# RWKV block with a split-precision feed-forward: the first tile's receptance input mixed ahead of its matmuls, tables loaded early, steps reordered

## The chip, the cores and the metric

The kernel runs on one core of a Trainium2 chip. The metric is device time in microseconds (us), the median of several runs. Beside the timed runs there is one profiled execution; all views of engines, waits and chains come from it.

## The reference, cut to what matters

`x` is 2 sequences of 4096 tokens with 256 features. A layernorm (without gain or bias) feeds a token-mixing attention, its result is added to `x`, a second layernorm feeds a feed-forward network, and that is added too.

```python
x_prev = jnp.pad(x[:, :-1, :], ((0, 0), (1, 0), (0, 0)))      # the token before
xk = x * time_mix_k + x_prev * (1.0 - time_mix_k)             # xv, xr alike
k = xk @ W_k.T; v = xv @ W_v.T; r = sigmoid(xr @ W_r.T)
# per token, with log-max state p and numerator q:
new_p = maximum(p, u + k_t)
scale_old = exp(maximum(p - new_p, -30)); scale_cur = exp(maximum(u + k_t - new_p, -30))
wkv_t = (scale_old * q + scale_cur * v_t) / (scale_old + scale_cur + 1e-9)
new_p2 = maximum(p + w, k_t)
q = exp(maximum(p + w - new_p2, -30)) * q + exp(maximum(k_t - new_p2, -30)) * v_t
y = r * wkv;  x = x + y @ W_o.T
# feed-forward of the second layernorm, width 1024, ternary weights with a scale per row:
h = silu(x2 @ w1.T * s1) * (x2 @ w2.T * s2)
h = gelu(h @ h1.T * sh1); h = gelu(h @ h2.T * sh2)
x = x + h @ w3.T * s3
```

## The kernel before, in words

Features lie on the 128 partitions (two blocks of 128, `ND = 2`), tokens on the free axis, in 16 tiles of 512 tokens. `split_block` does the work; `general_block` runs only if some feed-forward weight is not exact in the reduced format, which is tested on the way (`compare`) and isn't so here.

The feed-forward (`ffn`, lines 553 to 599) takes each input as the sum of a high and a low part (`hi`, `lo`), so that every product is two matmuls (lines 172 and 173). For tile i its steps are interleaved with the attention of tile i + 1 and the first layernorm of tile i + 2, generators that the loop at lines 608 to 624 advances step by step. A scheduler puts the emitted instructions into one queue per engine; every engine runs its queue in order. `tc.issue_after` ties an instruction behind another one.

The first tile has nothing to run beside, and so `first_tile` (lines 399 to 545) is written for latency, with the order on TensorE, VectorE and ScalarE fixed by hand: `on(engine, ...)` (line 340) puts every operation behind the one before on the same engine. Nearly all its operations therefore carry line 342. Its stages are:

- the first layernorm by halves of 256 tokens (`first_layernorm`, line 364), with dummy matmuls (`keep_warm`, line 356, output `unread`) in between;
- the token mix. It isn't applied to the tokens but to the weights: `scale` (line 431) makes, for k, v and r, copies `ws` of the 256x256 matrix whose rows are multiplied by the mix (`vec`) and by one minus the mix (`unmix`), four activations of 128x256 for each of the three. `project` (line 447) then needs four fp32 matmuls for each block: two with the tokens (`now`) and two with the tokens shifted by one (`then`);
- `differences` (line 464): a scan for the log-max (`state<-vec,state,ps_k`), and the exponents' arguments, clamped at line 472; `scales` (475): exp, relu, exp; two sigmoids for the shares `so`; a sigmoid of r; `state` (480): the numerator's scan and the two shares of the result;
- `y`, the output projection `ps_o`, the residual sum in `x_sb`, the second layernorm, and the split of `x2` into `x_hi` and `x_lo`, with which the feed-forward of tile 0 can start (its first matmul is `pa` at line 172).

Into this the steps of the second tile's first layernorm (`second = normalise(1)`) are placed by hand, one `next(second)` each: step 1 adds the halves and folds (`both` at line 187, a shift `folded` on ScalarE at 189), step 2 is the fold on VectorE (192) and `parts` on ScalarE (194), step 3 `parts` on VectorE (197), step 4 the averaging matmul (201), step 5 the subtraction (212), step 6 the variance, and so on. Step 1 also issues tile 2's load on GpSimd's queue. Steps 1 to 4 lie in `first_tile` (lines 491, 495, 508, 530), steps 5 and 6 in the feed-forward loop at steps 1 and 7, the rest at step 8 (lines 612 to 617).

GpSimd's queue issues the weight loads. After those of `w1`, `w2` and `h1` come eight copies of `h2` from HBM to HBM (line 123, 512 KB each), and the load of `w3` (124); behind these are the small copies `prev`, `log_max` and `numer` of the state that tile 1 needs (lines 445, 473, 484).

Of the kernel before, what the change touches and what calls it, by code (L numbers as in the profile page):

```python
# [13 lines left out]
P = 128  # L14
# [51 lines left out]
def split_block(ctx, tc, flags, x, vecs, w_attn, w1, w2, h1, h2, w3, out):  # L66
# [52 lines left out]
    h2_hbm = dram.tile([NH, P, NH, P], F32R, name="h2_hbm")  # L119
    for sb, src in ((w1_sb, w1), (w2_sb, w2), (h1_sb, h1)):  # L120
        nc.gpsimd.dma_start(out=sb, in_=src)
    for f in range(NH):
        nc.gpsimd.dma_start(out=h2_hbm[f], in_=h2[:, :, f * P : (f + 1) * P])
    nc.gpsimd.dma_start(out=w3_sb, in_=w3)

    mean_w = const.tile([P, P], F32, name="mean_w")
    vector.memset(mean_w, 1.0 / D)
# [209 lines left out]
    def behind(engine):  # L337
        return tc.issue_after(last[engine].ins) if engine in last else nullcontext()

    def on(engine, operation, *args, **kwargs):  # L340
        with behind(engine):
            last[engine] = getattr(getattr(nc, engine), operation)(*args, **kwargs)  # L342

    def matmul(*args, **kwargs):
        on("tensor", "matmul", *args, **kwargs)

    def activation(*args, **kwargs):
        on("scalar", "activation", *args, **kwargs)

    def add(out, a, b, op=ALU.add):  # L350
        on("vector", "tensor_tensor", out, a, b, op)

    def load_sqrt_table():
        activation(root, eps, AF.Sqrt)

    def keep_warm(unread, n, size=TS):

# [6 lines left out]
    def first_layernorm(src, xc, means):  # L364

        sq = wide.tile([P, ND, TS], F32, tag="wide", name="sq")
        for mean, p in zip(means, halves):
            for h in range(ND):  # L370
                add(xc[:, h, p], src[:, h, p], mean, ALU.subtract)
            activation(sq[:, :, p], xc[:, :, p], AF.Square)
        varis = []
        for p in halves:
            add(sq[:, 0, p], sq[:, 0, p], sq[:, 1, p])
            var = ps_ffn.tile([P, TS // 2 // P], F32, tag="pf", name="var")
            for b in range(TS // 2 // P):
                t = slice(p.start + b * P, p.start + (b + 1) * P)
                matmul(var[:, b : b + 1], sq[:, 0, t], mean_w[:, 0:1], start=True, stop=True)
            varis.append(var)  # L380
        yield
        spread = []
        for var in varis:
            each = tmp.tile([P, TS // 2 // P], F32, tag="each", name="each")
            activation(each, var, AF.Sqrt, bias=eps)
            on("vector", "reciprocal", each, each)
            rstd = ps_ffn.tile([P, TS // 2], F32, tag="pf", name="rstd")
            for b in range(TS // 2 // P):
                matmul(
                    rstd[:, b * P : (b + 1) * P], each[:, b : b + 1].to_broadcast([P, P]), ident, start=True, stop=True  # L390
                )
            spread.append(rstd)
            yield
        for rstd, p in zip(spread, halves):
            for h in range(ND):
                add(xc[:, h, p], xc[:, h, p], rstd, ALU.mult)
            yield

    def first_tile(second):
# [13 lines left out]
                    both = one.tile([P, 2, TS], F32, tag=tag, name="scale")  # L413
                    scales.append([both[:, k, :] for k in range(2)])

        load_sqrt_table()
        unread = ps_sum.tile([P, TS], F32, tag="ps", name="unread")
        keep_warm(unread, 8)
        means = []
# [6 lines left out]
        norm = first_layernorm(x_sb, xn, means)  # L426


        scaled = [[hid.tile([P, ND, D], F32, tag=tag, name="ws") for tag in ("hi", "lo")] for m in range(3)]

        def scale(m, *which):
            for k, c in which:
                j = m * ND + c
                activation(scaled[m][k][:, c, :], wa_sb[:, m, c, :], AF.Copy, scale=(vec, unmix)[k][:, j : j + 1])

        next(norm)
        scale(0, (0, 0))
        next(norm)
        scale(0, (1, 0))
        next(norm)  # L440
        scale(0, (1, 1), (0, 1))
        for m in range(1, 3):
            scale(m, (0, 0), (1, 0), (1, 1), (0, 1))
        run(norm)
        nc.gpsimd.tensor_copy(prev, xn[:, :, TS - 1 :])

        def project(m, h, kind, p=whole):
            pool, tag = kind
            ps = pool.tile([P, p.stop - p.start], F32, tag=tag, name="ps_" + "kvr"[m])
            now, then = (ws[:, :, h * P : (h + 1) * P] for ws in scaled[m])  # L450
            skip = 1 if p.start == 0 else 0
            shifted = slice(p.start + skip - 1, p.stop - 1)
            matmul(ps, now[:, 0, :], xn[:, 0, p], start=True, stop=False)
            for c in range(ND):
                matmul(ps[:, skip:], then[:, c, :], xn[:, c, shifted], start=False, stop=False)
            matmul(ps, now[:, 1, :], xn[:, 1, p], start=False, stop=True)
            return ps
# [6 lines left out]
        def differences(h):  # L464
            w, u = col(DECAY, h), col(FIRST, h)
            for k, p in keys[h]:
                t, after = lm[h][:, p], lm[h][:, p.start + 1 : p.stop + 1]
                on("vector", "tensor_tensor_scan", after, w.to_broadcast([P, p.stop - p.start]), k,
                   lm[h][:, p.start : p.start + 1], ALU.add, ALU.max)
                on("vector", "scalar_tensor_tensor", sc[h][1][:, p], t, w, k, ALU.add, ALU.subtract)  # L470
                on("vector", "scalar_tensor_tensor", so[h][1][:, p], k, u, t, ALU.add, ALU.subtract)
            on("vector", "tensor_scalar", sc[h][0], sc[h][1], NEG_CLAMP, 0.0, ALU.max, ALU.min)
            nc.gpsimd.tensor_copy(log_max[:, h : h + 1], lm[h][:, TS:])

        def scales(h):
            activation(sc[h][0], sc[h][0], AF.Exp)
            activation(sc[h][1], sc[h][1], AF.Relu)
            activation(sc[h][1], sc[h][1], AF.Exp, scale=-1.0)

        def state(h):  # L480

            on("vector", "scalar_tensor_tensor", sc[h][1], sc[h][1], MIN_SCALE, v[h], ALU.max, ALU.mult)
            on("vector", "tensor_tensor_scan", num[h][:, 1:], sc[h][0], sc[h][1], num[h][:, 0:1], ALU.mult, ALU.add)
            nc.gpsimd.tensor_copy(numer[:, h : h + 1], num[h][:, TS:])
            for share, of in zip(so[h], (num[h][:, 0:TS], v[h])):
                on("vector", "scalar_tensor_tensor", share, share, MIN_SHARE, of, ALU.max, ALU.mult)
            add(so[h][0], so[h][0], so[h][1])

        differences(0)
        with behind("vector"), behind("scalar"):  # L490
            next(second)
        last["vector"], last["scalar"] = marks["both"], marks["shift"]
        scales(0)
        with behind("vector"), behind("scalar"):
            next(second)
        last["vector"], last["scalar"] = marks["fold"], marks["hi"]
        differences(1)
        scales(1)
        for h in range(ND):
            activation(so[h][0], so[h][1], AF.Sigmoid, scale=-1.0)  # L500
            activation(so[h][1], so[h][1], AF.Sigmoid)
        for h in range(ND):
            activation(r[h], r[h], AF.Sigmoid)
            state(h)
        load_sqrt_table()

        with behind("vector"):
            next(second)
        last["vector"] = marks["split"]
        y = wide.tile([P, ND, TS], F32, tag="wide", name="y")  # L510
        add(y[:, 0, :], so[0][0], r[0], ALU.mult)
        for p in halves:
            add(y[:, 1, p], so[1][0][:, p], r[1][:, p], ALU.mult)
        banks = [
            [pool.tile([P, TS // 2], F32, tag=tag, name="ps_o") for pool, tag in kinds]
            for kinds in ((attn, attn), (attn, ffn))
# [6 lines left out]
        for ps_of, p in zip(banks, halves):  # L523
# [2 lines left out]
                add(x_sb[:, h, p], x_sb[:, h, p], ps_of[h])  # L526
                matmul(mean, mean_w, x_sb[:, h, p], start=h == 0, stop=h == ND - 1)
            means.append(mean)
        with behind("tensor"):
            next(second)  # L530
        last["tensor"] = marks["average"]
        unread = ps_attn.tile([P, TS], F32, tag="pa", name="unread")
        keep_warm(unread, 4)
        x2 = wide.tile([P, ND, TS], F32, tag="wide", name="x2")
        x2_hi = one.tile([P, ND, TS], F32R, tag="x2_hi", name="x2_hi")
        x2_lo = one.tile([P, ND, TS], F32R, tag="x2_lo", name="x2_lo")
        norm = first_layernorm(x_sb, x2, means)
        for _ in range(3):
            next(norm)
        keep_warm(unread, 6)  # L540
        run(norm)
# [63 lines left out]
    normal, got = {}, {}  # L605
    second = normalise(1)
    first_tile(second)
    for i in range(len(tiles)):
        ahead = attention(i + 1) if i + 1 < len(tiles) else iter(())
        further = normalise(i + 2) if i + 2 < len(tiles) else iter(())  # L610
        for step, _ in enumerate(ffn(i, *got.pop(i))):
            if i == 0:
                if step in (1, NH - 1):
                    with tc.issue_after(marks["rounded"].ins), tc.issue_after(marks["rest"].ins):
                        next(second)
                elif step == NH:
                    run(second)

            for _ in range(0 if step < NH else 4 if step == NH + (i == 0) else 1):
                next(ahead, None)  # L620
            if step > 2 * NH - 6 and step % 2 == 0:
                next(further, None)
        run(ahead)
        run(further)
# [287 lines left out]
```

## Time and profile before

| what | us |
|---|---|
| median of the timed runs (3) | 1572.11 |
| lowest and highest | 1571.52 and 1572.32 |
| the profiled execution, its own time | 1574.68 |
| its span | 1572.9 |
| PE busy | 1559.1 (99%) |
| DVE, ACT, POOL busy | 1102.0, 1034.4, 62.0 |
| first feed-forward matmul of tile 0 starts at | 45.14 |

PE is TensorE's matmuls, PEld its weight loads, DVE VectorE, ACT ScalarE, POOL GpSimd, SP SyncE. A line of the timeline gives start, duration, engine, source line, operation, output and inputs with their shapes, and in brackets the idle time before it and what ended it. A line of the chain gives start, duration, engine, output name and source line; it is followed back from the last instruction, so it shows who held up whom. The span starts at 0; a few us of the execution's own time lie outside it (1574.68 less 1572.9 is 1.8).

### The profile page before, as it was taken

What the parts mean: (1) busy time and instruction counts of PE and PEld (TensorE: products, weight loads), DVE (VectorE), ACT (ScalarE), POOL (GpSimd) and SP (SyncE); (2) the same over time, 40 slices, a digit from 0 to 9 for tenths busy, and PEclk for the clock granted to TensorE, in tenths of its full rate; (3) what the DMA queues carried; (4) which work ended last, traced back from release to release, by engine and by line L of the source; (5) the groups of instructions that cost most, each with busy time, mean ns of one, the idle gap of its engine ahead of it and who ended that gap; (6) DMA issues with size and microseconds to landing.
All of it is one profiled execution on the core that took longest, in us unless ns stands there. A gap on an engine that the chain in (4) does not pass through costs nothing.

```text
span 1572.9 us, 16652 instructions
## 1 busy us (share of the span) xinstructions
PE 1559.1 (99%) x6319; PEld 1185.9 (75%) x6319; DVE 1102.0 (70%) x1763; ACT 1034.4 (66%) x1394; POOL 62.0 (4%) x99
## 2 busy tenths in 40 slices
PE   9999999999999999999999999999999999999997
PEld 5768777777777778777787777877777787777886
DVE  6788686776768767786786867767687676865521
ACT  5676767667577585776767666675776857756542
POOL 3000000000000000000000000000000000000000
PEclk9999999999999999999999999999999999999999
DMA  9102031220402204021130311203112030211202
GB/s 360 42 32 103 14 121 34 73 88 9 130 30 75 79 20 134 14 90 65 34 121 14 107 48 47 94 14 108 41 64 78 21 108 27 80 48 34 94 14 69
DMA packets 36598, 109.16 MB, mean 69 GB/s; under 512 B 3680, under 2 KB 12384, under 8 KB 36000
## 3 DMA queue, kind: packets, MB, share of 16 engines
q1 hardware_dynamic: 19136, 67.93, 13.0%
q0 software_dynamic: 16960, 39.59, 8.1%
q8 instruction: 51, 0.84, 0.2%
q10 hardware_dynamic: 416, 0.52, 0.1%
q14 instruction: 35, 0.29, 0.1%
HBM read 99.64 MB, written 12.58 MB: 71 GB/s over the span
## 4 chain that ended last, share of the span: by engine, by line
PE 80%; issue 15%; DVE 2%; ACT 1%; DMA 1%; POOL 0%; POOLq 0%; DVEq 0%
PE ph L172 24%; PE ph L173 24%; PE pb L172 3%; PE pa L172 3%; PE pb L173 3%; PE pa L173 3%; PE po L173 3%; PE po L172 3%; PE ps_k L165 3%; PE ps_r L165 3%; PE ps_v L165 3%; PE ps_o L165 3%; PE mean L201 1%; DVE scale L342 0%; PE var L201 0%
## 5 line engine op out<-in xcount | busy, mean ns | idle before, releaser
L172 PE MATMUL ph<-hi,h_sb 128*128 128x512 f32 x2048 | 813.8, 397 | 0.0
L173 PE MATMUL ph<-lo,h_sb 128*128 128x512 f32 x2048 | 801.4, 391 | 0.0
L172 PEld LDWEIGHTS ph<-hi,h_sb 128*128 128x128 f32 x2048 | 384.9, 188 | 92.7 <-issue 11.7
L173 PEld LDWEIGHTS ph<-lo,h_sb 128*128 128x128 f32 x2048 | 385.0, 188 | 88.6 <-issue 8.4
L583 DVE TENSOR_TENSOR lo<-full,hi 128x512 fp32r<-128x512 f32 x256 | 175.4, 686 | 174.7 <-ACT full L582 173.6
L580 ACT ACTIVATE hi<-ph,vec 128x512 fp32r<-128x512 f32 x256 | 175.7, 686 | 183.3 <-PE ph L173 181.9
L582 ACT ACTIVATE full<-ph,vec 128x512 f32<-128x512 f32 x256 | 174.2, 681 | 0.9 <-DVE lo L583 0.8
L565 DVE SCALAR_TENSOR_TENSOR gated<-pb,vec,gated 128x512 f32<-128x512 f32 x128 | 95.5, 748 | 58.2 <-PE pb L173 31.0
L580 ACT ACT_TABLE_LOAD x102 | 130.9, 1283 | 1.8
L564 ACT ACTIVATE gated<-pa,vec 128x512 f32<-128x512 f32 x128 | 86.5, 684 | 59.7 <-PE pa L173 56.5
L220 DVE RECIPROCAL rstd<-rstd 128x512 f32<-128x512 f32 x30 | 100.4, 3346 | 5.3 <-ACT rstd L218 5.3
L172 PE MATMUL pb<-x_hi,w_sb 128*128 128x512 f32 x256 | 102.1, 399 | 0.6 <-DVE gated L565 0.6
L172 PE MATMUL pa<-x_hi,w_sb 128*128 128x512 f32 x256 | 102.0, 398 | 0.1
L173 PE MATMUL pb<-x_lo,w_sb 128*128 128x512 f32 x256 | 100.7, 393 | 0.0
L173 PE MATMUL pa<-x_lo,w_sb 128*128 128x512 f32 x256 | 100.6, 393 | 0.0
L173 PE MATMUL po<-lo,w_sb 128*128 128x512 f32 x256 | 100.3, 392 | 0.0
L172 PE MATMUL po<-hi,w_sb 128*128 128x512 f32 x256 | 100.1, 392 | 0.0
L179 ACT ACTIVATE hi<-gated 128x512 fp32r<-128x512 f32 x128 | 80.6, 630 | 27.9 <-DVE gated L565 26.5
L180 DVE TENSOR_TENSOR lo<-gated,hi 128x512 fp32r<-128x512 f32 x128 | 87.7, 686 | 5.3 <-ACT hi L179 0.7
L248 DVE TENSOR_TENSOR_SCAN lm<-vec,lm,ps_k 128x512 f32<-128x512 f32 x30 | 38.3, 1278 | 42.9 <-PE ps_k L165 42.8
L303 DVE SCALAR_TENSOR_TENSOR mx<-xn,vec,mx 128x512 f32<-128x512 f32 x90 | 66.4, 744 | 0.3
L595 DVE SCALAR_TENSOR_TENSOR x_sb<-po,vec,x_sb 128x512 f32<-128x512 f32 x32 | 24.0, 751 | 58.9 <-PE po L173 58.9
(144 smaller groups left out, 1815.8 us busy)
## 6 DMA issues: line engine op xcount, KB each, us to landing
h_sb<-h_hbm SPq DMA_DIRECT2D x128, 512.0 KB, 3.3
out<-x_sb POOLq DMA_DIRECT2D x16, 512.0 KB, 3.1
raw<-in_h POOLq DMA_DIRECT2D x32, 256.0 KB, 3.1
x_sb<-in_x POOLq DMA_DIRECT2D x15, 512.0 KB, 4.1
h_sb<-in_h POOLq DMA_DIRECT2D x1, 4096.0 KB, 20.6
h_hbm<-in_h POOLq DMA_DIRECT2D x8, 512.0 KB, 22.9
w_sb<-in_w POOLq DMA_DIRECT2D x3, 1024.0 KB, 11.4
raw<-in_w POOLq DMA_DIRECT2D x12, 256.0 KB, 2.8
```

The costliest lines, as they stand in the source:

```text
L165: tensor.matmul(psum, weights(c), src[c], start=c == 0, stop=c == n - 1)
L172: tensor.matmul(psum, weights(c), hi, start=c == 0, stop=False)
L173: tensor.matmul(psum, weights(c), lo, start=False, stop=c == n - 1)
L179: marks["rounded"] = scalar.activation(hi, full, AF.Copy)
L180: marks["rest"] = vector.tensor_tensor(lo, full, hi.bitcast(F32), ALU.subtract)
L220: vector.reciprocal(rstd, rstd)
L303: vector.scalar_tensor_tensor(mx[:, h, :], xn[:, h, 1:], vec[:, j : j + 1], mx[:, h, :], ALU.mult, ALU.add)
L564: scalar.activation(full, pa, AF.Silu, scale=col(S1, f))
L565: vector.scalar_tensor_tensor(full, pb, col(S2, f), full, ALU.mult, ALU.mult)
L580: scalar.activation(hi, ps, AF.Gelu, scale=col(scales, f))
L582: scalar.activation(full, ps, AF.Gelu, scale=col(scales, f))
L583: vector.tensor_tensor(lo, full, hi.bitcast(F32), ALU.subtract)
```

## The change

For r in the first tile, the tokens are mixed instead of the weights: ScalarE makes `mx` (tokens times mix) and `then` (shifted tokens times one minus mix), four activations of 128x512, and GpSimd adds the two, 128x511, twice. The four weight copies of r go, and so do half of r's matmuls: two for each block, with the plain weights. ScalarE loads the exponential's table right after this. `prev`, `log_max` and `numer` copies stand in the order given to GpSimd, and the `h2` copies and the load of `w3` are issued behind them (`load_rest`). Of the second tile's layernorm only step 1 stays in `first_tile`, now behind the last `y`; steps 2 to 5 go into the feed-forward's steps 0 to 3. The first half's `y` (feature block 0) stands between the second block's scan and its shares. In the first layernorm the variance of the halves is two steps, with two dummy matmuls of 128 columns between them.

```diff
-    for f in range(NH):
-        nc.gpsimd.dma_start(out=h2_hbm[f], in_=h2[:, :, f * P : (f + 1) * P])
-    nc.gpsimd.dma_start(out=w3_sb, in_=w3)
+    def load_rest():
+        for f in range(NH):
+            nc.gpsimd.dma_start(out=h2_hbm[f], in_=h2[:, :, f * P : (f + 1) * P])
+        nc.gpsimd.dma_start(out=w3_sb, in_=w3)
...
             varis.append(var)
-        yield
+            yield
...
-        scaled = [[hid.tile([P, ND, D], F32, tag=tag, name="ws") for tag in ("hi", "lo")] for m in range(3)]
+        scaled = [[hid.tile([P, ND, D], F32, tag=tag, name="ws") for tag in ("hi", "lo")] for m in range(2)]
...
+        next(norm)
+        keep_warm(unread, 2, P)
         next(norm)
         scale(0, (0, 0))
...
-        for m in range(1, 3):
-            scale(m, (0, 0), (1, 0), (1, 1), (0, 1))
+        scale(1, (0, 0), (1, 0), (1, 1), (0, 1))
         run(norm)
-        nc.gpsimd.tensor_copy(prev, xn[:, :, TS - 1 :])
+        mx, then = (wide.tile([P, ND, TS], F32, tag="wide", name="mx") for _ in range(2))
+        for c in range(ND):
+            j = 2 * ND + c
+            activation(mx[:, c, :], xn[:, c, :], AF.Copy, scale=vec[:, j : j + 1])
+            activation(then[:, c, 1:], xn[:, c, : TS - 1], AF.Copy, scale=unmix[:, j : j + 1])
+            on("gpsimd", "tensor_tensor", mx[:, c, 1:], mx[:, c, 1:], then[:, c, 1:], ALU.add)
+        load_table(AF.Exp)
+        on("gpsimd", "tensor_copy", prev, xn[:, :, TS - 1 :])
...
+            if m == 2:
+                for c in range(ND):
+                    matmul(ps, wa_sb[:, 2, c, block], mx[:, c, :], start=c == 0, stop=c == ND - 1)
+                return ps
...
-        differences(0)
-        with behind("vector"), behind("scalar"):
-            next(second)
-        last["vector"], last["scalar"] = marks["both"], marks["shift"]
-        scales(0)
-        with behind("vector"), behind("scalar"):
-            next(second)
-        last["vector"], last["scalar"] = marks["fold"], marks["hi"]
-        differences(1)
-        scales(1)
+        for h in range(ND):
+            differences(h)
+            scales(h)
         for h in range(ND):
             activation(so[h][0], so[h][1], AF.Sigmoid, scale=-1.0)
             activation(so[h][1], so[h][1], AF.Sigmoid)
         for h in range(ND):
             activation(r[h], r[h], AF.Sigmoid)
-            state(h)
-        load_sqrt_table()
-        with behind("vector"):
-            next(second)
-        last["vector"] = marks["split"]
+        load_table(AF.Sqrt)
         y = wide.tile([P, ND, TS], F32, tag="wide", name="y")
-        add(y[:, 0, :], so[0][0], r[0], ALU.mult)
+        state(0)
+        result(0)
+        state(1)
+        add(y[:, 0, :], so[0][0], r[0], ALU.mult)
+        result(1)
         for p in halves:
             add(y[:, 1, p], so[1][0][:, p], r[1][:, p], ALU.mult)
+        with behind("vector"), behind("scalar"):
+            next(second)
+        last["vector"], last["scalar"] = marks["both"], marks["shift"]
...
-        with behind("tensor"):
-            next(second)
-        last["tensor"] = marks["average"]
...
+    with behind("gpsimd"):
+        load_rest()
...
-                if step in (1, NH - 1):
+                if step in (0, 1, 2, 3, NH - 1):
```

`state` is cut in two: `state` keeps the product and the scan, `result` has the two shares and their sum.

More of the change, by code (lines that the diff above doesn't have):

```diff
@@ L351, in add, with load_table @@
         on("vector", "tensor_tensor", out, a, b, op)
-    def load_sqrt_table():
-        activation(root, eps, AF.Sqrt)
+    def load_table(function):
+        activation(root, eps, function)
     def keep_warm(unread, n, size=TS):
@@ L449, in project @@
             ps = pool.tile([P, p.stop - p.start], F32, tag=tag, name="ps_" + "kvr"[m])
-            now, then = (ws[:, :, h * P : (h + 1) * P] for ws in scaled[m])
+            block = slice(h * P, (h + 1) * P)
+            if m == 2:
+                for c in range(ND):
+                    matmul(ps, wa_sb[:, 2, c, block], mx[:, c, :], start=c == 0, stop=c == ND - 1)
+                return ps
+            now, then = (ws[:, :, block] for ws in scaled[m])
             skip = 1 if p.start == 0 else 0
@@ L472, in differences @@
             on("vector", "tensor_scalar", sc[h][0], sc[h][1], NEG_CLAMP, 0.0, ALU.max, ALU.min)
-            nc.gpsimd.tensor_copy(log_max[:, h : h + 1], lm[h][:, TS:])
+            on("gpsimd", "tensor_copy", log_max[:, h : h + 1], lm[h][:, TS:])
         def scales(h):
@@ L483, in state, with result @@
             on("vector", "tensor_tensor_scan", num[h][:, 1:], sc[h][0], sc[h][1], num[h][:, 0:1], ALU.mult, ALU.add)
-            nc.gpsimd.tensor_copy(numer[:, h : h + 1], num[h][:, TS:])
+            on("gpsimd", "tensor_copy", numer[:, h : h + 1], num[h][:, TS:])
+        def result(h):
             for share, of in zip(so[h], (num[h][:, 0:TS], v[h])):
@@ L503, in first_tile @@
             activation(r[h], r[h], AF.Sigmoid)
-            state(h)
-        load_sqrt_table()
-        with behind("vector"):
-            next(second)
-        last["vector"] = marks["split"]
+        load_table(AF.Sqrt)
         y = wide.tile([P, ND, TS], F32, tag="wide", name="y")
+        state(0)
+        result(0)
+        state(1)
         add(y[:, 0, :], so[0][0], r[0], ALU.mult)
+        result(1)
         for p in halves:
             add(y[:, 1, p], so[1][0][:, p], r[1][:, p], ALU.mult)
+        with behind("vector"), behind("scalar"):
+            next(second)
+        last["vector"], last["scalar"] = marks["both"], marks["shift"]
         banks = [
@@ L537, in first_tile @@
         norm = first_layernorm(x_sb, x2, means)
-        for _ in range(3):
+        for _ in range(4):
             next(norm)
```

## Prediction

> **What bounds the kernel now.** I read the page's busy row first, then who keeps PE waiting once the feed-forward runs, then the chain of the first 46 us, and last the timeline and the granted clock inside that stretch.
>
> ```profile
> PE 1559.1 (99%) x6319; PEld 1185.9 (75%) x6319; DVE 1102.0 (70%) x1763; ACT 1034.4 (66%) x1394; POOL 62.0 (4%) x99
> ```
>
> The waits of PE's matmuls between 45 and 1565 us hold one entry:
>
> ```profile
> PE pb L172 <- DVE gated L565: 0.6, 1, 0.6
> ```
>
> So from the first feed-forward matmul at 45.14 us the kernel is a row of matmuls without gaps, and its order hardly changes: on PE one averaging matmul comes in, and two neighbours swap. What the change is worth is read ahead of 45.14, one for one, plus what it adds to that row. The chain there (start, us, engine, output):
>
> ```profile
> 9.56 1.50 PE rstd L342 x8
> 11.06 4.91 PE ps_k L342 x16
> 15.99 0.76 DVE state L342
> 16.78 1.21 DVE scale L342 x3
> 17.99 0.61 DVE both L187
> 18.62 0.64 ACT folded L189
> 19.28 0.68 DVE folded L192
> 19.97 1.20 DVE state L342
> ...
> 26.08 0.64 ACT scale L342
> 26.74 1.36 DVE scale L342 x2
> 28.13 1.30 DVE scale L342 x2
> 29.45 1.30 DVE state L342
> 30.84 1.30 DVE scale L342 x2
> 32.17 0.69 DVE scale L342
> 32.89 0.70 DVE parts L197
> 33.61 0.70 DVE y L342
> 34.35 3.72 PE ps_o L342 x16
> 38.07 1.74 PE mean L342 x8
> ```
>
> The second tile's steps (`both`, `folded`, `parts`) stand in the first tile's chain, and `ps_o`, 16 entries for 8 matmuls, runs whole behind the first `y`. r's matmuls (26.08 to 33.1) end just before `y`, and are not in it.
>
> **The change, part by part.**
>
> Two dummy matmuls. Eleven of them took 6.43 to 8.17, 0.158 each, so 0.32; PE idles 0.18 at that place (waiting for `sq`, before 8.96). Cost: +0.14 on everything behind. Whether they do something for the clock comes below.
>
> ScalarE. Four weight copies go (about 0.4 each, start to start); four activations of 128x512 come in. `sq`, as large, took 0.63: 2.5 us. k's and v's copies end near 12.3, so these end near 14.9, and the exponential's table (1.28, and 0.20 for its dummy) near 16.4. The first exp needs the clamp that ended at 17.99: hidden, with 1.6 to spare. This table load stood at 19.27 to 20.55 before, also beside other work, so loading it earlier gains nothing by itself.
>
> GpSimd's adds. No row shows a GpSimd add. The nearest is the 128x128 select, 0.31, which at four times the length is 1.24; with two inputs up to twice that, 2.5. The Trainium skill (GPSIMD Engine Reference, section 3.1) speaks against moving such work: an add of 2048 fp32 took 4.5 us there, twice VectorE's; a quarter of that is an estimate of 1.1. I take 1.2: the adds end near 14.9 and 16.1; with 2.5, near 18.7. r's matmuls need them at 26.2. Both ends are hidden; below zero it can't go. The dearer question is VectorE, which shares a way into memory:
>
> ```profile
> 29.45 1.29 DVE L342 TENSOR_TENSOR_SCAN state<-scale,state 128x512 f32<-128x512 f32 x1
> ...
> 29.48 1.22 POOL L473 COPY log_max<-state 128x1 f32<-128x1 f32 x1
> ```
>
> A one-column copy, 0.17 at 27.42, took 1.22 and ended with VectorE's scan. The skill (SBUF — State Buffer, "Who interferes with whom") calls this an exclusive lock for whole instructions, met by VectorE operations with two inputs in SBUF or in a two-port mode. By that rule, what VectorE does from 13.6 to 17.6 (scans and differences of `ps_k`, one input in PSUM) isn't touched; the clamp (0.42, at 17.57) is, if an add still runs. Were every VectorE operation held instead, block 0 would slip by up to 1.2, and it has 1.5 in hand, since block 1's keys come only at 19.5. Zero either way, while an add is near 1.2.
>
> The second tile's steps. `both` and `folded` go from the stretch 17.99 to 19.97. What is late next is k's block 1: `ps_k` ends at 10.86 + 8.53 = 19.39, plus 0.14 and some 0.04 to be seen, 19.57. The scan started at 19.89: gain 0.32, not the two steps' 1.3. The clamp (ended 22.94) and the exps behind it move by that; `parts` on ScalarE ended at 22.89, so it held nothing. v's block 0 comes at about 23.0, and its numerator is through at 25.0, before the sigmoids. The sigmoid's table and sigmoids stay, the shares start at 26.74 - 0.32 = 26.42.
>
> From the shares to `y`. Block 1's scan starts at 29.13 and ends at 30.42. New behind it: tile 1's two one-column copies, drawn here by the scheduler (durations 0.15 and 0.14, I count 0.25), and `y` of block 0 (0.61 start to start). Block 1's shares start at 31.28. Before, from there to the next `y` took 33.61 - 30.84 = 2.77, of which `parts` 0.72; so 2.05, and `y` of block 1, first half, starts at 33.33 and ends at 33.75. Until 33.2 PE has done block 0's four output matmuls (each 3.57 / 8 = 0.446). Sigmoids of r: its 8 entries of 0.43 end near 29.8, hidden.
>
> Output and mean. PE has four matmuls left from 33.79 to 35.57, then two of the first half's mean, 0.89, and 0.16 to be seen: VectorE's subtraction at 36.62. Before: 34.35 + 3.57 + 0.89 + 0.16 = 38.97, which is where the trace has it. Gain 2.35. `both` (0.69) now stands ahead of the residual sums, which start at 34.65 instead of 34.4; their second ends at 35.5, when PE wants it at 36.0. Hidden, by half a us; without that cover it would cost 0.3.
>
> From there to 45.14 nothing but `mean`'s averaging matmul goes, which was in no chain. The feed-forward starts at 42.8.
>
> In the feed-forward: that matmul adds 0.23 to a full PE (start to start of a 512-column one). VectorE gets `folded` and `parts` (0.68 each), ScalarE one `parts` (0.61) in steps 0 to 2, the subtraction (1.28) moves from step 1 to 3. Behind them wait `gated` and `lo`, and for those PE's banks, two steps ahead. Laying the new order out with the trace's durations, the averaging matmul finds its input 0.3 ready, and `pb` of step 7 its bank just freed: 0 to 0.3 of stall, I take 0.
>
> GpSimd's queue. Nine issues (0.75 and 0.55) and tile 2's load (0.73) now start near 30.6, when the second `numer` copy is done. VectorE isn't slowed by them: its share at 26.74 took 0.69 beside the issue at 26.36. `h2`'s copies, 4 MB, need about 12 us at the 350 GB/s of the first 40 us, up to 25 as both read and write count: landed by 56, `w3` by 60; layer 2 and `w3` are wanted after 90 and near 138. Nothing, as long as GpSimd gets there. SP's first read of them waits, and nothing is queued behind it that is wanted sooner.
>
> Sum: -2.35 + 0.23 = -2.12. The profiled execution would take 1574.68 - 2.12 = 1572.6; the timed runs lie 2.6 lower, and I subtract from their median: 1570.0.
>
> **The clock.** The windows of that stretch (columns: window, its length, busy PE, PEld, DVE, ACT and POOL, clock, DMA share, GB/s):
>
> ```profile
> 9.00:10.00 1.00, 1.00 (x8) 0.92 (x8) 0.27 (x2) 0.87 (x4) 0.78 (x2) 1.00 1.07 428
> 11.00:12.00 1.00, 1.00 (x4) 0.82 (x3) 0.75 (x2) 1.00 (x4) 0.00 (x0) 0.50 1.00 401
> 12.00:13.00 1.00, 1.00 (x4) 0.74 (x4) 0.00 (x0) 1.00 (x4) 0.22 (x1) 0.50 1.22 492
> ```
>
> From 10.4 to 13.6 the granted clock is half, and k's first block runs at half speed: 3.15 us for 1.57 of work. The skill (TensorE: Matmul & The Clock Gate, "Why this matters for your kernels") wants no idle gap above some 3 us; by that rule PE, 82% or more busy, should not be gated, and two dummies change nothing. The row says it was, so what counts must be finer, and short matmuls seem to count little. Two of 128 columns are 2 x 0.229 / 4 = 0.11 of array work, 3% of the 3.4 us ahead of the gate. That is little to tip it. If it does, k's block 1 comes 1.57 sooner, and all behind it can follow: the table is ready at 16.4, its first user now at about 16.4.
>
> **The rivals.**
> - The gate stays away. For: half clock inside the bounding chain, and dummies put where it is decided. Against: 3%. -2.12 - 1.57 = -3.7: 1568.4.
> - A part of the gain is lost: PE idles about 1.5 us from 29.8 to 31.4 and again ahead of 33.8, where before r filled it; a half clock there would stretch 3.4 us of output and mean by up to 1.7. Or GpSimd's first add has a start-up of some us and holds the clamp. For: the gate above came without idle gaps. Against: `ps_o` is dense work. -2.1 + 1.7 = -0.4; I put 1571.7.
> - Slower: the adds are long and hold the lock. If one takes d from 13.65, the second ends at 13.65 + 2d, and block 1's clamp, due at 22.6, waits for it. From d = 4.5 it costs, from 5.5 it eats the 2.1; at d = 7 it is 13.65 + 14 - 22.6 = 5.0 lost: 1575.0. For: no row shows such an add. Against: a select of a quarter the size took 0.31.
> - The table and r do nothing of themselves: that is my forecast already.
>
> **How the numbers follow.** My forecast has 0.55; the gate stays away 0.23; partly lost 0.14; slower 0.08. This kernel's measurements tell about 0.2%, 3.1 us, from no change. The forecast, -1.7 to -2.6, lies inside it but for 0.03; the gate's case lies beyond. Faster 0.23 + 0.03 = 0.26, slower 0.08, same 0.66. The range: from 1567.7 (the gate's case with the spread of the timed runs, 0.4 either way, and as much for my sums) to 1572.4 (all lost).
>
> **What would show it.** The first `pa` near 42.8, block 1's scan near 19.6, the shares at 26.4, the first half's `y` near 33.3, adds of about 1.2 us ending before 17; the clock half from about 10.4. I am wrong if adds take over 4 us and the clamp waits, if the clock falls after 30, or if PE waits for `gated` or `parts` in the first eight steps.

## The result, and the profile after

| | before | changed |
|---|---|---|
| median, runs side by side on one chip (22 each) | 1572.84 | 1569.78 |
| lowest and highest | 1571.52, 1574.98 | 1568.79, 1571.86 |
| ratio, 95% interval | | 0.9981 [0.9975, 0.9986] |
| the profiled execution, its own time | 1574.68 | 1569.95 |
| first feed-forward matmul `pa` (us from the span's start) | 45.14 | 40.76 |

The change takes 3.06 us off, at the edge of what counts here as a difference. The forecast time, 1570.0, was met; the change itself is larger than the 1.7 to 2.6 that were forecast, and the first feed-forward matmul moved further still (4.38). That has to be taken apart before the sum can be called right.

The busy row of after, for the row of before: five us less of PE, nothing else of note.

```profile
PE 1554.0 (99%) x6313; PEld 1181.3 (75%) x6313; DVE 1101.6 (70%) x1763; ACT 1036.3 (66%) x1395; POOL 63.5 (4%) x101
```

PE's waits between 41 and 1565 us have no entry now (before: one of 0.6). So the feed-forward is still a row without gaps, and the change is again to be read ahead of `pa`. The chain of after there (start, us, engine, output, line):

```profile
10.48 7.13 PE ps_k L344 x24
17.64 1.29 DVE state L344
...
24.50 1.36 DVE scale L344 x2
...
27.21 1.29 DVE state L344
28.60 0.59 DVE y L344
...
31.22 0.43 DVE y L344
...
33.69 1.74 PE mean L344 x8
...
40.76 0.50 PE pa L174
```

`both`, `folded` and `parts` are out of it, `y` of block 0 stands between the second scan and its shares. The timeline of after has the new work (in brackets the idle time before an entry, and what ended it):

```profile
13.21 2.49 POOL L344 TENSOR_TENSOR mx<-mx 128x511 f32<-128x511 f32 x2 [8.53 <-ACT mx L344]
...
24.30 3.60 PE L344 MATMUL ps_r<-mx,wa_sb 128*128 128x512 f32 x8
29.30 1.97 PE L344 MATMUL ps_o<-y,wa_sb 128*128 128x256 f32 x8 [1.40 <-issue]
31.70 1.99 PE L344 MATMUL ps_o<-y,wa_sb 128*128 128x256 f32 x8 [0.44 <-DVE y L344]
...
49.49 0.39 PE L203 MATMUL mean<-parts,mean_wr 128*128 128x512 f32 x1
```

The adds take 1.25 each and end at 15.7, 8.6 ahead of r's matmuls; these are half as many; and the averaging matmul in the feed-forward finds its input ready. Behind the last `y`, `ps_o` is 8 entries where it was 16. All that is as forecast. One thing isn't: in the windows of after (busy PE, PEld, DVE, ACT, POOL, then the clock) the clock that fell to 0.50 before stays at 1.00.

```profile
11.00:12.00 1.00, 1.00 (x6) 0.90 (x5) 0.32 (x1) 1.00 (x4) 0.00 (x0) 1.00 1.08 432
12.00:13.00 1.00, 1.00 (x7) 0.87 (x6) 0.52 (x1) 1.00 (x2) 0.00 (x0) 1.00 1.10 442
```

That looks like the rival of the gate: two dummies that keep the clock up. The experiments first ask whether it is.

### The profile page after: what moved, and what is told of

It reads as the page before. It is cut to its first block, busy times and chain, and to the rows that moved or that the text cites. A ratio compares the mean times of both kernels' runs of the same rounds, so it can differ in the third digit from the quotient of the medians.

```text
span 1568.2 us, 16639 instructions
## 1 busy us (share of the span) xinstructions
PE 1554.0 (99%) x6313; PEld 1181.3 (75%) x6313; DVE 1101.6 (70%) x1763; ACT 1036.3 (66%) x1395; POOL 63.5 (4%) x101
## 4 chain that ended last, share of the span: by engine, by line
PE 81%; issue 15%; DVE 2%; ACT 1%; DMA 0%; POOL 0%; POOLq 0%; DVEq 0%
PE ph L174 24%; PE ph L175 24%; PE pa L174 3%; PE pb L174 3%; PE pb L175 3%; PE pa L175 3%; PE po L175 3%; PE po L174 3%; PE ps_k L167 3%; PE ps_r L167 3%; PE ps_v L167 3%; PE ps_o L167 3%; PE mean L203 1%; PE var L203 0%; PE ps_k L344 0%
```

## The experiments

Two theories: **P**, the prediction's sum (the gain is the moved steps, the early `y` and the shorter r; whether the clock dips early is another matter), and **G**, the gate's rival (the two dummies keep the clock full). Kernels are given by their difference from before or from the changed kernel. All were timed beside before, in three sets, each on one chip; of one (e6_exp_not_preloaded) there is only the profiled execution.

What makes small differences readable here is that each run's record also has its mean granted clock. A stretch of 3.4 us at half clock costs 1.7 in 1570, or 0.001 of that mean. Of the 14 profiled executions five have 0.997, and these five all show such a stretch; the nine with 0.998 or more show none (in two of the five, the late `y` and the early issues below, it lies behind 28 us and not at the start). Behind the last matmul all 14 have another 4.3 to 7.5 us at half clock, for which nothing waits; it moves the mean by up to 0.001 too, so that a single run at the border can be sorted wrongly. With that reserve runs are sorted by it: "full" below is 0.998 and more, "dipped" 0.997 or less. Before's 107 runs of the three sets fall into 55 full ones with a median of 1572.07 and 52 dipped ones with 1573.91.

### Who keeps the clock: the two dummies taken out, and put into before

From the changed kernel (e1_no_dummies):

```diff
-        keep_warm(unread, 2, P)
```

Into before (e2_before_dummies):

```diff
-        yield
+            yield
...
+        keep_warm(unread, 2, P)
+        next(norm)
```

> The changed kernel without the two dummy matmuls between the halves' variances. In the changed kernel's profile the clock was full from 8 to 16 us, in the profile of before it was half from 10.4 to 13.6. Theory G (the two dummies keep the clock up): half clock near 10 to 13 again, k's block 1 about 1.5 us later, and a time of about 1571.3 (the changed kernel's 1569.8 plus 1.57). Theory P (the clock's dip comes and goes from one execution to the next, whatever the dummies do): a time within 0.4 of the changed kernel's, 1569.4 to 1570.2, and a profile that may show either clock.

> The kernel before with the two dummy matmuls alone. Theory G: no dip of the clock, about 1.4 us less than before (0.9991). Theory P: 0.14 more than before, not to be told from it (1.0000), and a profile that may show either clock.

Measured: without the dummies 1569.03 (0.4 under the range expected of P), 0.9977 [0.9969, 0.9986], clock full in its profile, 3 of 12 runs dipped. Before with them: 1572.36, 1.0000 [0.9992, 1.0008]; its profile has the dip (0.55, 0.50, 0.50, 0.75 in the windows from 10 to 14), and 6 of 13 runs have it. G falls: the dummies neither keep the clock nor does it fall without them. The profile after simply was an execution without the dip, and that of before one with it.

### The parts alone: the steps of the second tile, and r

Before, with steps 1 to 4 taken from where they stood, and step 1 behind the last `y` (e3_steps_moved):

```diff
+        with behind("vector"), behind("scalar"):
+            next(second)
+        last["vector"], last["scalar"] = marks["both"], marks["shift"]
...
-                if step in (1, NH - 1):
+                if step in (0, 1, 2, 3, NH - 1):
```

The changed kernel with r as before, from scaled weights, without the mix and the adds (e4_r_by_weights):

```diff
-        scale(1, (0, 0), (1, 0), (1, 1), (0, 1))
+        for m in range(1, 3):
+            scale(m, (0, 0), (1, 0), (1, 1), (0, 1))
...
-            on("gpsimd", "tensor_tensor", mx[:, c, 1:], mx[:, c, 1:], then[:, c, 1:], ALU.add)
...
-            if m == 2:
```

> The kernel before with only the second tile's layernorm steps moved as in the change: step 1 behind the last y, steps 2 to 5 in the feed-forward's steps 0 to 3. By the prediction's sums: k's block 1 is taken up 0.46 sooner and 'parts' (0.72) goes, but r's eight matmul entries for each block end at 33.1 and the output matmuls queue behind them, so these start at 33.15 instead of 34.35: 1.2 less, plus 0.23 for the averaging matmul in the feed-forward: about 1.0 less than before (0.9994). Rival: the steps alone hold all of the prediction's 2.1 (0.9987), and r's shorter way gives nothing.

> The changed kernel with r taken from scaled weights as before (eight matmuls instead of four, no ScalarE mix, no GpSimd adds; all else as changed). By the prediction's sums r's matmuls then end 3.4 us later and the first half of the output matmuls queues behind them on TensorE, so the output's second half starts 1.3 us later than in the changed kernel: about 1571.1. Rival (r's matmuls are hidden, as they were before): the time of the changed kernel, 1569.8.

Measured: the steps alone 1572.1, 0.9994 [0.9986, 1.0003]; everything but r 1571.03, 0.9992 [0.9985, 0.9998]. The first alone can't be told from no change, though its median lies 0.6 under before's of that set and the forecast, 1.0, was of that order. In both, `ps_o` starts only when r's sixteen entries are through (30.88 and 30.71) and runs as one group; with r by weights:

```profile
23.85 7.02 PE L344 MATMUL ps_r<-xn,ws 128*128 128x512 f32 x16
30.71 3.62 PE L344 MATMUL ps_o<-y,wa_sb 128*128 128x256 f32 x16
```

So r's mixing buys nothing where it stands, but clears PE for `ps_o`: against before of their own set, full runs with r by weights gain 1.23 and dipped ones 1.25, those of the changed kernel (repeated below, in another set) 2.59 and 2.84. The difference, 1.4 to 1.6, is r's by the runs. The profiles price it as well. Their starts differ (the first variance matmul comes anywhere from 7.50 to 8.20), and some have the early dip; both drop out of the distance from the second block's scan to `pa`:

| profile | scan of block 1 | `pa` | apart |
|---|---|---|---|
| before (dipped) | 19.89 | 45.14 | 25.25 |
| before, dense dummies (below, no dip) | 18.37 | 43.62 | 25.25 |
| the steps alone | 17.25 | 41.67 | 24.42 |
| r by weights | 17.19 | 41.40 | 24.21 |
| changed | 17.64 | 40.76 | 23.12 |

There r is worth 1.1, where the forecast for it was 1.3.

### The early y: put back behind the second block's shares, with and without filling

In the changed kernel (e5_y_late):

```diff
-        add(y[:, 0, :], so[0][0], r[0], ALU.mult)
         result(1)
+        add(y[:, 0, :], so[0][0], r[0], ALU.mult)
```

The same, and behind r's projection (e12_y_late_filled):

```diff
+        keep_warm(unread, 12)
```

> The changed kernel with the first block's y back behind the second block's shares (all else as changed). By the prediction's sums the first four output matmuls, 1.8 us, then start where the last y starts instead of 1.9 us sooner, and the other four queue behind them: about 1.3 us more than the changed kernel, 1571.1. Rival (VectorE, not the output matmuls, sets the pace there): the time of the changed kernel, 1569.8.

> The changed kernel with the first block's y late, and twelve dummy matmuls of 512 columns behind r's, which fill TensorE's gap of 3.5 us there. If the late y cost 4.2 mostly by the clock, what is left is the queueing of the output matmuls, 1.3 by the prediction's sums: about 1571.1, clock full from 28 to 37. Rival (the late y costs 4 by itself): 1573.9.

Measured: 1573.94, 1.0002 [0.9993, 1.0011], so 4.2 over the changed kernel where 1.3 was expected. With the filling 1571.78, 0.9991 [0.9982, 1.0000]. Two lines of the first, from the timeline and from the windows, then the same window of the filled one:

```profile
31.26 5.38 PE L344 MATMUL ps_o<-y,wa_sb 128*128 128x256 f32 x16 [3.54 <-issue]
```

```profile
33.00:34.00 1.00, 1.00 (x4) 0.77 (x3) 0.00 (x0) 0.09 (x1) 1.00 (x3) 0.50 1.69 315
```

```profile
33.00:34.00 1.00, 1.00 (x7) 0.87 (x6) 0.08 (x1) 0.32 (x1) 1.00 (x3) 1.00 1.52 280
```

PE idles 3.54 and then runs `ps_o` and `mean` at half clock for 3.4 us; with the gap filled the clock stays at 1.00 throughout, and `pa` starts 1.38 after that of the changed kernel's repetition beside it (42.25 and 40.87), which is the queueing that was forecast. The runs sort the same way: of the eleven with `y` late, two have no dip (1570.7, 1.1 over full runs of the changed kernel), three have one (1572.62) and six have two, a mean clock of 0.996 (1574.53). Each dip costs 1.9. The filled kernel's full runs lie 1.9 over the repetition's, 0.5 more than its `pa` explains; that half us (nine runs against five) is open.

### The table, and GpSimd's queue

In the changed kernel (e6_exp_not_preloaded):

```diff
-        load_table(AF.Exp)
```

In the changed kernel, the nine issues ahead of the adds, where before has them (e7_rest_early):

```diff
+    load_rest()
...
-    with behind("gpsimd"):
-        load_rest()
```

> The changed kernel without the early dummy exp. ScalarE has nothing between 14.4 and the first clamp, so the load of the exponential's table should run in the same gap or at the latest in front of the first exp, and the second block's exps, which bound the stretch, start when their clamp ends either way: the first feed-forward matmul within 0.1 of the changed kernel's for the same clock. Rival (the early load is what gains): it starts 1.3 us later.

> The changed kernel with the h2 copies and w3's load issued early, as before, ahead of the adds on GpSimd's queue. Before, that queue waited for transfers until 26.9; so the adds would run from 26.9 to 29.4 instead of 13.2 to 15.7, r's first block would end at 31.2 and y of block 0, which stands in VectorE's fixed order ahead of the second block's shares, would start at 31.9 instead of 28.5: 3.4 us more than the changed kernel, 1573.2. Rival (r has slack enough, the move of the loads is only tidiness): within 0.4 of 1569.8.

Measured in one execution: 1570.24 without the early table. Its `pa` starts at 41.02, 0.26 after that of the profile after, but so does its first variance matmul (8.20 and 7.94); from the scan to `pa` both take 23.12. ScalarE's timeline shows why the early load isn't missed:

```profile
14.75 1.28 ACT L344 ACT_TABLE_LOAD   x1
16.54 1.81 ACT L344 ACTIVATE scale<-scale 128x512 f32<-128x512 f32 x3 [0.51 <-DVE scale L344]
```

The load starts right behind the mix's activations and is over 0.51 before the clamp's result comes, for which the exponential waits: it doesn't wait with it. With the issues ahead of the adds: 1573.24, 0.9999 [0.9990, 1.0008]. That is 3.5 over the changed kernel, where 3.4 was expected, in part by luck, as the lines show. Its timeline:

```profile
26.90 2.48 POOL L346 TENSOR_TENSOR mx<-mx 128x511 f32<-128x511 f32 x2
...
26.92 3.56 DVE L346 TENSOR_TENSOR_SCAN state<-scale,state 128x512 f32<-128x512 f32 x1
...
28.23 4.97 PE L346 MATMUL ps_r<-mx,wa_sb 128*128 128x512 f32 x7 [4.06 <-POOL mx L346]
```

The adds come at 26.90, r waits for them, PE idles 4.06 and its clock is half from 28.5 to 31.9, so that `y` of block 0 starts at 32.43 instead of the 31.9 expected. And a scan with both inputs in SBUF, 1.29 elsewhere, takes 3.56 while the adds run: the exclusive lock of the Trainium skill (SBUF — State Buffer, "Who interferes with whom"), this time at VectorE's cost. Neither the half clock nor the held scan was in the expectation. The order in GpSimd's queue is a part of the change without which it gains nothing.

### Long adds

In the changed kernel, six more adds on values that nothing reads any more (e8_adds_long):

```diff
+        for c in (0, 1, 0, 1, 0, 1):
+            on("gpsimd", "tensor_tensor", then[:, c, 1:], then[:, c, 1:], then[:, c, 1:], ALU.add)
```

> The changed kernel with six more GpSimd adds of the same size behind the two (on the second operand, whose value is not used any more), so that GpSimd adds from 13.2 to some 23. Lock as the skill's rule has it: of VectorE's operations only the two clamps (and those with two inputs in SBUF) wait for the add under way, at most 1.25 each; the first clamp has 1.4 in hand, the second is on the path: 0 to 1.25 more than the changed kernel, about 0.6, 1570.4. Rival, every VectorE operation waits: the scans and differences of the second block too, several us more, over 1572. Second rival, nothing waits: 1569.8.

Measured: 1571.47, 0.9989 [0.9980, 0.9998]; 8 of 11 runs dipped, and so is its profile, which is why the median lies above the 1570.4 expected. Against full runs of the changed kernel its three full ones are 0.9 slower, against its dipped ones its eight 0.4. Its timeline:

```profile
13.47 8.66 POOL L344 TENSOR_TENSOR mx<-mx 128x511 f32<-128x511 f32 x8 [8.78 <-ACT mx L344]
...
14.17 0.75 DVE L344 TENSOR_TENSOR_SCAN state<-vec,state,ps_k 128x256 f32<-128x256 f32 x1 [2.32 <-PE ps_k L344]
...
17.48 0.78 DVE L344 TENSOR_SCALAR scale<-scale 128x512 f32<-128x512 f32 x1
...
21.97 0.44 DVE L344 TENSOR_SCALAR scale<-scale 128x512 f32<-128x512 f32 x1
```

Under the adds the scans that read PSUM keep their 0.75, while block 0's clamp takes 0.78 instead of 0.42: the prediction's reading of the lock by kinds of operation holds. In this dipped execution block 1's clamp, at 21.97, comes as the last add ends (22.13) and takes its usual time; in a full one it comes 1.7 sooner, under them, which agrees with the 0.9 of three runs but isn't seen in a trace.

This profile is worth more as a picture of the changed kernel with the dip: up to `ps_k` it starts like the profile of before (10.86), and its chain has

```profile
19.33 1.29 DVE state L344
...
26.22 1.36 DVE scale L344 x2
...
42.48 0.50 PE pa L174
```

where the forecast wrote 19.6, 26.4 and 42.8.

### The dip taken out of both, and the changed kernel again

In before and in the changed kernel alike (e9_before_dense, e10_after_dense), with the variance as two steps in both:

```diff
-        keep_warm(unread, 11, P)
+        keep_warm(unread, 4)
...
         next(norm)
+        keep_warm(unread, 1)
         next(norm)
+        keep_warm(unread, 1)
```

Four dummies of 512 columns take the place of eleven of 128, and one of 512 behind each half's variance that of two of 128 or none. Beside them ran e11_after_again, the changed kernel itself.

> The kernel before with denser dummy matmuls in the first layernorm: four of 512 columns instead of eleven of 128, and one of 512 behind each half's variance. If the early dip of the clock comes from too little array work in the stretch ahead of it, no execution dips: the times leave out the upper half of the runs of before (1573 to 1575), and the median is that of its lower half, about 1571.8. Rival (the dip has nothing to do with the work given): both halves as before, median 1572.8. If the dummies stand in the way, more than that.

> The changed kernel with the same denser dummies. If array work is what counts, all runs lie where 17 of 22 of the changed kernel lay (1568.8 to 1570.5), none at 1571.3 to 1571.9, median about 1569.5, which beats the changed kernel's by little. Rival: a fifth to a quarter of the runs stay up there.

> The changed kernel itself, on the same chip as the others of this call: median 1569.8, with some runs near 1571.6, where the clock dips early; if the profiled one is such a run, its first feed-forward matmul is near the forecast's 42.8, otherwise near 40.8.

Measured: before 1572.25, 0.9993 [0.9984, 1.0002]; changed 1569.83, 0.9977 [0.9967, 0.9986]; the changed kernel again 1570.35, 0.9982 [0.9973, 0.9991]. None of the 21 runs with dense dummies is dipped; of the runs beside them, 16 of before's 32 and 6 of the changed kernel's 11 are. Windows of before and of the changed kernel with dense dummies:

```profile
11.00:12.00 1.00, 1.00 (x6) 0.87 (x6) 0.60 (x2) 1.00 (x4) 0.00 (x0) 1.00 1.05 420
```

```profile
11.00:12.00 1.00, 1.00 (x5) 0.90 (x6) 0.80 (x3) 1.00 (x4) 0.00 (x0) 1.00 1.08 434
```

With the dip out of both, this is the cleanest measure of the change: `pa` goes from 43.62 to 41.24, -2.38; the issue of the first output's DMA from 141.96 to 139.83, -2.13; the profiled executions' own times from 1571.75 to 1569.71, -2.04; the medians by -2.42.

Why one run dips and the next doesn't can be read from the profiles. Two windows of before:

```profile
10.00:11.00 1.00, 1.00 (x7) 0.89 (x6) 0.81 (x3) 1.00 (x4) 0.72 (x1) 0.72 1.09 430
...
1565.00:1573.00 8.00, 0.00 (x0) 0.00 (x0) 0.00 (x0) 0.00 (x0) 0.00 (x0) 0.62 0.21 75
```

A mean clock of 0.72 means that the last 0.56 us of this window are at half clock, which therefore starts at 10.44; in the same way the half clock behind the last matmul starts at 1566.9. In finer windows the five profiles with a dip have:

| profile | dip starts | last half clock starts | apart | in steps of 3.4133 |
|---|---|---|---|---|
| before | 10.44 | 1566.91 | 1556.47 | 456.0 |
| before with two dummies | 10.10 | 1566.57 | 1556.47 | 456.0 |
| long adds | 10.25 | 1563.32 | 1553.07 | 455.0 |
| late `y` | 32.64 | 1565.22 | 1532.58 | 449.0 |
| early issues | 28.50 | 1564.49 | 1535.99 | 450.0 |

Each of the five dips lasts 3.41; the distances differ from each other by 3.40, 17.08 and 3.41, which is one, five and one times that; and each is a whole number of such steps. So in these traces the clock changes only at points 3.41 us apart, and where these points lie differs from one execution to the next. Counted back from the last half clock, one of them lies at 10.1 to 10.4 in the three profiles with the early dip. In the nine others with thin dummies one lies at 8.0 to 9.2 (the next 3.41 later) or, once, at 10.66, and there is no early dip. In the changed kernel with dense dummies one lies at 10.29, among those that dipped, and the clock stays at 1.00. So the early dip seems to take both, a thin stretch and such a point at its end. That is a reading of 14 profiles; no run moves the points at will.

## Why the prediction was right

The forecast's case happened: the sum was -2.12, and with the clock alike on both sides the change is worth -2.42 (medians with dense dummies; -2.04 in their profiles), -2.44 (full runs of all sets together) and -2.68 (dipped ones). The 3.06 of the two medians has another half us in it, which is a matter of mixture: before's runs are half dipped, so that its median falls between the two groups, and 12 of the changed kernel's 33 are, so that its median falls in the lower one. Whether the change makes dips rarer isn't settled: 12 of 33 against 52 of 107 is 1.2 standard errors. That the time itself fits so well has some luck in it: the sum was taken from 1572.11, the median of three runs that all lie near the full ones' 1572.07, so that 1570.0 was in effect a forecast for full runs (1569.6), and most of the runs behind the changed kernel's median happened to be full.

Step by step, forecast against the long adds' profile, which has the dip as the forecast assumed: block 1's scan 19.57, 19.33; shares 26.42, 26.22; the first half's `y` 33.33, 32.95; subtraction 36.62, 36.32; `pa` 42.8, 42.48. Each comes 0.2 to 0.4 early. In the profile after, without the dip, all lie 1.9 to 2.1 earlier, and the distances between them are kept: scan to shares 6.86 (forecast 6.85), shares to `y` 6.72 (6.91), `y` to subtraction 3.37 (3.29), subtraction to `pa` 6.17 (6.17).

- **The terms of the sum.** The averaging matmul costs 0.23 in the forecast; from `pa` to the first output's issue before takes 98.30, after 98.55 (98.34 and 98.59 with dense dummies). The two dummies were put at +0.14 and cost nothing on the path: from the first variance matmul to `pa` 32.82 us go by with them and 32.83 without. The two one-column copies were put at 0.25; from the scan's start at 27.21 to `y` at 28.60 there are 1.39, no more than lay before between this scan and the operation behind it (29.45 to 30.84). These two make up most of the 0.2 to 0.4 by which the steps come early. A term was also misread: the row of half clock was taken to end at 13.6 and to cost 1.57, but it lasts until 13.85 and costs 1.7; the sum doesn't contain it.
- **Costed at nothing.** ScalarE's four activations (11.80 to 14.35), the table, the adds, r's sigmoids, `both` ahead of the residual sums, the late issues: no wait on any of them in the trace after. For the issues that rests on their new place: left in the old one, ahead of the adds, they cost the whole gain.
- **r.** Its shorter matmuls were in no chain of before, and the sum had them only as "Until 33.2 PE has done block 0's four output matmuls". The runs price that at 1.4 to 1.6, the profiles at 1.1: about half of the gain can't be had without it.
- **The early y.** Rightly seen as letting `ps_o` start before the last `y`. What the forecast didn't see is that it also keeps PE's gap at 1.40; late, the gap is 3.54 and half clock follows, by the sorting in at least six of eleven runs and in up to nine. The rival of the partly lost gain priced such a dip at up to 1.7 after 29.8 (1.9 measured), but hung it on the wrong gap: after 1.40 and 0.44 the clock stays.
- **The gate.** The row was read as a property of before. It is one of an execution: with the kernel unchanged, half the runs have it. The Trainium skill's rule against idle gaps above some 3 us (TensorE: Matmul & The Clock Gate, "Why this matters for your kernels") agrees with the gaps of 3.54 and 4.06 here; it doesn't cover the early dip, where PE was 82% busy or more. That "short matmuls seem to count little" is what the dense dummies bear out: the same place, filled with 512 columns at a time, had no dip in 21 runs.
- **The slower rival** needed adds of 4.5 us. They take 1.25, and eight in a row 1.08 each, near the estimate of 1.1 from the Trainium skill's GPSIMD Engine Reference, section 3.1.

## What to carry to other kernels

A gain of two us in a kernel whose clock falls to half for 3.4 us in some runs and not in others can't be read from two profiles: sort the runs by their granted clock, or fill the place with dense matmuls in both kernels, and compare like with like. When work is taken off PE ahead of a wait, look at how long the gap becomes, since the matmuls behind it may pay for it at half speed; here an early first `y` kept it short, and 512-column dummies did as well. The changed kernel with dense dummies (1569.83) is no faster in its best runs than the changed kernel, but it has no dipped ones.

## What the runs showed of the hardware that was not expected

- The clock fell to half after PE idled 3.54 and 4.06 us, not after 1.40, and also, in about half the runs of before, in a stretch without such a gap, made of 128-column and one-column matmuls. What tips it from run to run, by the profiles, is where the points lie at which the clock changes, 3.41 us apart. The first `mean` matmuls go with it: the four took 1.93 to 2.08 in the three profiles with the early dip and in the two others with a point at 10.29 or 10.66, and 1.09 to 1.49 in the remaining nine. Nor need a gap fill such a step: of the 3.54, only 2.03 lie in the 3.41 us ahead of the dip at 32.64.
- GpSimd's add and VectorE's scan with SBUF inputs exclude each other, and by these two cases the one that comes first makes the other pay: a one-column copy waited a us for the scan before, and the scan waited 2.3 for the adds when they were moved.
- A table load ran ahead of the wait of the activation that needs it (14.75, 1.79 before that activation), so that loading it by a dummy gained nothing while ScalarE was idle.
